# Local attention on one NeuronCore: the product with swapped halves in one VectorE instruction, and the inverse root written straight into the norms' tile

## The chip, the cores and the metric

The program runs on one NeuronCore of a Trainium2 chip, as one launch. The metric is device time in microseconds (us); lower is better. A NeuronCore has four engines that compute: TensorE (PE in the profile; its weight loads are shown apart as PEld), VectorE (DVE), ScalarE (ACT) and GpSimd (POOL). A fifth, SyncE (SP), issues most of the transfers. Each engine takes its own instructions strictly in order; an instruction that waits holds up everything behind it on that engine.

## The reference, cut to what matters

The program is a stack of eight stages (four attention layers, four feed-forward layers) over an activation of 4 sequences x 512 positions x 128 channels, with a residual sum and a layer norm after each stage. The change lies in the second stage alone, a two-layer local attention with eight heads of 64 channels. The part that matters:

```python
def l2norm(t):
    return t / jnp.clip(jnp.linalg.norm(t, axis=-1, keepdims=True), 1e-12)

def rotate_half(x):
    x1, x2 = jnp.split(x, 2, axis=-1)
    return jnp.concatenate([-x2, x1], axis=-1)

def rotary_xpos(q, k):
    ...
    q = q * cos * scale + rotate_half(q) * sin * scale
    k = k * cos / scale + rotate_half(k) * sin / scale
    return (q, k)

def _layer(x, wqkv, qs, ksc, wo, lg, lb, w1, b1, w2, b2):
    ...
    qkv = h @ wqkv
    q, k, v = jnp.split(qkv, 3, axis=-1)
    q, k, v = (to_heads(q), to_heads(k), to_heads(v))
    q = l2norm(q) * qs
    k = l2norm(k) * ksc
    q, k = rotary_xpos(q, k)
    o = local_attention(q, k, v)
    ...
    h = a * jax.nn.gelu(g, approximate=False)
    x = x + h @ w2 + b2
    return x
for l in range(DEPTH):
    x = _layer(x, wqkv[l], q_scale[l], k_scale[l], ...)
```

Queries and keys are divided by their norms, scaled, and rotated: each vector times a cosine table, plus the vector with its two halves of 32 swapped times a sine table.

## The kernel before, in words

The stages run one behind the other on one core, and overlap at their seams: the next stage's loads and first operands are made while the last one ends. Local attention is class `F0`. It works through eight *units* (two layers x four sequences), and in each unit through eight *heads*, so 64 heads in all. Three streams of work are interleaved:

- `qkv(u)` makes the operands of unit u. For each of four chunks of 128 positions it multiplies by the weights of q, k and v (`mm3`, three matmuls each). For q and for k, ScalarE copies the product out of PSUM into a tile (`ta` for q, `kr` for k; line 1616) and squares it into `sq` (line 1619). VectorE then makes the sine product `tb` (line 1623, **two** instructions, one for each half: the output's first half reads the input's second half and the other way round), the cosine product in place (line 1625) and the sum of squares of each head (line 1626). For q the two products are added on TensorE, by two accumulating transposes; for k GpSimd adds them (line 1633), and the sum is transposed later. When all four chunks are through, `rsqrt` turns the 64 sums of squares of each partition into inverse norms, in ten short VectorE steps that each need the one before (lines 342 to 353), and line 1647 copies the result into the tile `rn`. Line 1653 multiplies the keys by it; the queries' norms are applied later, as a scalar of the scores (line 1689).
- `scores` and `score` work off the heads: TensorE makes scores (line 1676), VectorE adds the band mask and takes the minimum (line 1689, four instructions of 128x128 for a head, out to `sm` and `nb`), ScalarE takes the exponential (line 1691, four a head). `turn` transposes and copies (line 1701), `values` multiplies by v (line 1720). `sm` has one buffer (`ns = 1`), so a head's mask has to wait for the exponentials of the head before.
- `post(u)` is what follows the attention of a unit: divide by the sums (line 1753), project (1759), add (1761), shift by transfers (1764 and 281), normalise, and a feed-forward with a Gelu on ScalarE (line 1800, one instruction of 128x1024 and one of 85x512) and a last sum (1817 or 1820).

Exponential and Gelu use different function tables of ScalarE. At each change between them the compiler puts a table load (ACT_TABLE_LOAD in the profile, under the line of the function that needs it).

The order on each engine is not written out by hand. The program yields steps of these streams in turn; each instruction has a priority from its place in the program, and a scheduler that keeps clocks of its own puts the instructions of all streams in one order for each engine when the program is built. A change of an instruction can so move others that it has nothing to do with. `rsqrt` is also called for the layer norms (`norm`, with four columns in place of 64).

Inside the stage, time 243 to 635 us is where the heads are worked off (line 1676 first starts at 243.4 us); before it unit 0's operands are made under the first stage, and behind it the last two `post` run into the third stage, of which some lines appear below (line 276 loads `a1kvs`, line 946 on GpSimd makes `qt`, line 949 on VectorE reduces it).

Of the kernel before, what the change touches and what calls it, by code (L numbers as in the profile page):

```python
# [12 lines left out]
ALU = mybir.AluOpType  # L13
# [3 lines left out]
P = 128  # L17
# [22 lines left out]
class K:  # L40
# [292 lines left out]
        nc.vector.tensor_tensor(l, ps, h.bitcast(F32), ALU.subtract)  # L333
        return h, l, f

    def rsqrt(self, pool, v, n, bufs=2):

        nc = self.nc
        t = pool.tile([P, 3, n], F32, tag=f"rs{n}", name=f"rs{self.uid}", bufs=bufs)
        self.uid += 1  # L340
        y, a, b = t[:, 0, :], t[:, 1, :], t[:, 2, :]
        nc.vector.tensor_scalar(a.bitcast(I32), v.bitcast(I32), 1, None, ALU.logical_shift_right)
        nc.vector.tensor_scalar(y.bitcast(I32), a.bitcast(I32), -1.0, float(0x5F3759DF), ALU.mult, ALU.add)
        nc.vector.tensor_tensor(a, y, y, ALU.mult)
        nc.vector.tensor_tensor(b, a, v, ALU.mult)
        yield
        nc.vector.tensor_scalar(a, b, 0.375, -1.25, ALU.mult, ALU.add)
        nc.vector.tensor_tensor(a, a, b, ALU.mult)
        nc.vector.scalar_tensor_tensor(y, a, 1.875, y, ALU.add, ALU.mult)
        yield  # L350
        nc.vector.scalar_tensor_tensor(a, y, -0.5, y, ALU.mult, ALU.mult)
        nc.vector.tensor_tensor(b, a, v, ALU.mult)
        nc.vector.scalar_tensor_tensor(y, b, 1.5, y, ALU.add, ALU.mult)
        return y

    def norm(self, r, X):
# [456 lines left out]
class Rel(Attn):  # L813
# [28 lines left out]
    def weights(self):  # L842
        k, d, pool = self.k, self.k.d, self.early
        h, l, fill = k.split_w(pool, d["a1_w3"], 384, "a1w", raw=("t1", 2))
        qkv = k.load(pool, d["a1_qkv"], [P, 384], "a1qkv")
        wo = k.load(pool, d["a1_wo"], [P, P], "a1wo")
        bo = k.bcast(pool, d["a1_bo"], P, "a1bo")
        ub = k.bcast(pool, d["a1_uv"][0], P, "a1ub")
        uv = k.load(pool, d["a1_uv"].rearrange("a p -> p a"), [P, 3], "a1uv")
        self.last = k.load(pool, d["c_last"], [P, 1], "a1last")  # L850
        self.w = dict(h=h, l=l, qkv=qkv, o=wo, bo=bo, ub=ub, uv=uv)
        yield from fill
# [640 lines left out]
class F0:  # L1493
# [83 lines left out]
    def qkv(self, u, X, tag="t"):  # L1577

        k, nc, pool = self.k, self.nc, self.more
        own = self.pool if u % 2 else pool  # L1580
        wait = k.turn if u == 0 else lambda: ()
        l, b = divmod(u, NB)
        w = self.w
        xh, xl = self.xs
        if l == 0:
            nc.sync.dma_start(self.x0[b], X)
        yield from k.turn()
        ps = k.bank("b")
        for c in range(4):
            k.tr(ps[:, c * P:(c + 1) * P], X[:, c, :])  # L1590
        yield

        for r, o in ((slice(0, 64), 0), (slice(64, P), 1)):
            nc.scalar.copy(xh[r, o:T + o], ps[r])
            nc.vector.tensor_tensor(xl[r, o:T + o], ps[r], xh[r, o:T + o].bitcast(F32), ALU.subtract)
        qT = own.tile([P, 4, T], F32, tag="qT", name=f"qT{u}")
        kT = own.tile([P, 4, 64 + T], F32, tag="kT", name=f"kT{u}")
        nc.gpsimd.memset(kT[:, :, 0:64], 0.0)
        v = own.tile([P, 4, 512], F32, tag="v", name=f"v{u}")
        kr = pool.tile([P, 4, 512], F32, tag="kr", name=f"kr{u}", bufs=1)  # L1600
        ss = pool.tile([P, 2, 4, 8], F32, tag="ss", name=f"ss{u}", bufs=2)
        for _ in range(2):
            yield
        for c in range(4):
            cs = slice(c * P, (c + 1) * P)
            for s in range(3):
                yield from wait()
                ps = k.bank("b")
                ws = slice(512 * s, 512 * s + 512)
                k.mm3(ps, xh[:, cs], xl[:, cs], w["qkvh"][:, ws], w["qkvl"][:, ws])  # L1610
                if s == 2:
                    nc.scalar.copy(v[:, c, :], ps)
                    yield
                    continue
                x = kr[:, c, :] if s else pool.tile([P, 512], F32, tag="ta", name=f"ta{u}{c}", bufs=self.nta)
                nc.scalar.copy(x, ps)
                yield
                sq = pool.tile([P, 512], F32, tag="sq", name=f"sq{u}{c}{s}", bufs=1)
                nc.scalar.activation(sq, x, AF.Square)
                tb = pool.tile([P, 8, 64], F32, tag="tb", name=f"tb{u}{c}{s}", bufs=2)  # L1620
                x3 = x.rearrange("p (h d) -> p h d", d=64)
                for a, b2 in ((0, 32), (32, 0)):
                    nc.vector.tensor_tensor(tb[:, :, a:a + 32], x3[:, :, b2:b2 + 32],
                                            w["tab"][:, 2 * s + 1, c, None, a:a + 32].to_broadcast([P, 8, 32]), ALU.mult)
                nc.vector.tensor_tensor(x3, x3, w["tab"][:, 2 * s, c, None, :].to_broadcast([P, 8, 64]), ALU.mult)
                nc.vector.tensor_reduce(ss[:, s, c, :], sq.rearrange("p (h d) -> p h d", d=64), AX.X, ALU.add)
                yield
                for _ in range(self.wait_ta if u == 0 else 0):
                    yield
                if s == 0:  # L1630
                    q = x3, tb
                else:
                    nc.gpsimd.tensor_tensor(x3, x3, tb, ALU.add)

            yield from wait()
            t = k.bank(tag)
            for pr in range(4):
                for j, y in enumerate(q):
                    k.tr(t[:, pr * P:(pr + 1) * P], y[:, 2 * pr:2 * pr + 2, :].rearrange("p h d -> p (h d)"), start=(j == 0), stop=(j == 1))
            nc.scalar.copy(qT[:, :, cs], t.rearrange("p (a n) -> p a n", n=P))  # L1640
            yield

        sf = ss.rearrange("p s c h -> p (s c h)")
        nc.vector.tensor_scalar(sf, sf, 1e-24, None, ALU.max)
        rn = pool.tile([P, 2, 4, 8], F32, tag="rn", name=f"rn{u}", bufs=2)
        y = yield from k.rsqrt(pool, sf, 64, 1)
        nc.vector.tensor_copy(rn.rearrange("p s c h -> p (s c h)"), y)
        for _ in range(self.wait_rn - 2):
            yield
        for c in range(5):  # L1650
            if c < 4:
                kc = kr[:, c, :].rearrange("p (h d) -> p h d", d=64)
                (nc.gpsimd if self.pk else nc.vector).tensor_tensor(kc, kc, rn[:, 1, c, :, None].to_broadcast([P, 8, 64]), ALU.mult)
                yield
            if c:
                yield from wait()
                t = k.bank(tag)
                for pr in range(4):
                    k.tr(t[:, pr * P:(pr + 1) * P], kr[:, c - 1, pr * P:(pr + 1) * P])
                nc.scalar.copy(kT[:, :, 64 + (c - 1) * P:64 + c * P], t.rearrange("p (a n) -> p a n", n=P))  # L1660
        self.S[u] = (qT, kT, v, rn)
# [729 lines left out]
```

## Time and profile before

| | |
|---|---|
| median of 3 runs | 2247.07 us (2244.59, 2247.07, 2247.89) |
| the profiled execution's own time | 2249.67 us |
| its span, first to last instruction | 2247.6 us |
| mean granted clock of TensorE | 0.965 |
| VectorE busy in the span | 1669.2 us in 5592 instructions |
| line 1623: count, median duration | 128 (half products of 128x256), 418 ns for q and 416 ns for k |
| line 1625: count, median duration | 64 (128x512), 683 ns for q and 682 ns for k |
| line 1647: count, median duration | 8 (128x64), 193 ns |
| table loads of ScalarE in local attention's heads (243 to 635 us) | 12 (6 for Gelu, 6 for the exponential), 1283 ns each |

All durations are of one profiled execution. A duration runs from an instruction's start to its end; neighbours on VectorE overlap a little, so what an instruction takes of the engine is the distance to the next one's start.

### The profile page before, as it was taken

To read this page: it belongs to the slowest core of one execution; us is meant where nothing else is said; L and a number is where in the kernel's file an instruction comes from. 1 tells how busy PE (TensorE), PEld (TensorE's weight loads), DVE (VectorE), ACT (ScalarE), POOL (GpSimd) and SP (SyncE) were. 2 spreads that over 40 slices of the span, in tenths; PEclk is the share of its full clock that TensorE was granted. 3 is DMA by queue.
4 is the path that set the end of the run, shared out by engine and by line. 5 is a ranking of instruction groups with operands and counts; after the bars stand their busy time and mean duration, and the time that the engine had idled before them with its cause. 6 is when DMAs were issued, how large, how long until landed. Compare 5 with 4: busy or idle time off the path is not lost.

```text
span 2247.6 us, 43130 instructions
## 1 busy us (share of the span) xinstructions
PE 2025.6 (90%) x14400; PEld 1472.7 (66%) x14400; DVE 1669.2 (74%) x5592; ACT 1331.7 (59%) x2982; POOL 504.3 (22%) x707
## 2 busy tenths in 40 slices
PE   7999888888878999999999999998999899999897
PEld 4566566676656667676887665776666566666676
DVE  5778688888878676873777775553877877778787
ACT  3566787777734666665333666332877777777632
POOL 3222212111211532433000322531111111111220
PEclk9999999999988999999999999998999999999999
DMA  5321312021433454321021420603889888888400
GB/s 170 106 77 35 102 49 62 8 48 27 116 113 94 143 157 140 113 79 56 16 66 40 117 78 21 218 17 90 209 213 210 203 196 190 195 206 204 104 5 15
DMA packets 264919, 242.10 MB, mean 108 GB/s; under 512 B 106353, under 2 KB 190619, under 8 KB 263867
## 3 DMA queue, kind: packets, MB, share of 16 engines
q1 hardware_dynamic: 259466, 221.86, 37.0%
q0 software_dynamic: 5232, 17.50, 3.3%
q8 instruction: 115, 1.88, 0.4%
q14 instruction: 106, 0.86, 0.1%
HBM read 103.82 MB, written 74.32 MB: 79 GB/s over the span
## 4 chain that ended last, share of the span: by engine, by line
PE 59%; DVE 17%; ACT 9%; DMA 7%; issue 4%; POOL 2%; SPq 1%; ACTq 0%; POOLq 0%; DVEq 0%
PE t L219 5%; PE s L2113 4%; PE o L737 3%; PE s L688 3%; PE t L721 3%; PE o L1377 3%; PE o L1016 3%; PE b L219 3%; PE b L311 3%; PE o L2009 2%; PE s L311 2%; PE b L313 2%; PE b L312 2%; PE s L313 2%; PE s L312 2%
## 5 line engine op out<-in xcount | busy, mean ns | idle before, releaser
L969 DVE CUSTOM_DVE_ANT_0 junk<-w,a1mask 128x640 bf16<-128x640 f32 x256 | 202.9, 817 | 66.3 <-PE w L967 64.4
L219 PE MATMUL t<-ident,p 128*128 128x128 f32 x1280 | 200.6, 278 | 26.4 <-ACT p L1334 17.3
L765 ACT ACTIVATE Pt<-t 128x384 f32<-128x384 f32 (+1 forms) x384 | 179.6, 528 | 67.4 <-PE t L721 55.7
L219 PEld LDWEIGHTS t<-ident,p 128*128 128x128 f32 x1280 | 151.2, 141 | 83.5 <-ACT p L1334 38.3
L1347 ACT COPY PT<-t 128x512 f32<-128x512 f32 x256 | 149.9, 595 | 76.2 <-PE t L219 75.3
L1043 ACT ACTIVATE Pt<-t 128x512 f32<-128x512 f32 x256 | 149.1, 597 | 73.4 <-PE t L1042 44.4
L1334 ACT ACTIVATE p<-s,nb 128x512 f32<-128x512 f32 x256 | 178.2, 700 | 12.4 <-DVE nb L1333 6.7
L1333 DVE TENSOR_REDUCE nb<-s 128x1 f32<-128x512 f32 x256 | 174.4, 685 | 2.5
L690 DVE CUSTOM_DVE_ANT_0 junk<-s,a0mask 128x128 bf16<-128x128 f32 (+3 forms) x256 | 114.1, 484 | 45.9 <-PE s L688 45.0
L1352 DVE CUSTOM_DVE_ANT_0 jk<-p,a3right 128x496 bf16<-128x496 f32 (+3 forms) x256 | 124.6, 487 | 26.9 <-ACT p L1334 14.8
L690 DVE CUSTOM_DVE_ANT_0 junk<-s,a2mask 128x128 bf16<-128x128 f32 (+3 forms) x256 | 114.8, 483 | 30.5 <-PE s L688 30.4
L774 POOL TENSOR_SCALAR_AFFINE_SELECT Pt<-Pt 128x512 f32<-128x512 f32 x112 | 70.0, 637 | 256.4 <-ACT Pt L765 256.3
L1331 DVE TENSOR_TENSOR s<-s,W 128x160 f32<-128x160 f32 (+1 forms) x256 | 80.9, 317 | 62.5 <-PE s L1329 61.2
L1328 PE MATMUL s<-a3KT,a3QT 128*128 128x512 f32 x256 | 118.7, 466 | 5.6 <-DVE nb L1333 2.5
L1377 PE MATMUL o<-PT,V 128*64 128x512 f32 x512 | 116.9, 598 | 0.5 <-ACT PT L1347 0.5
L1691 ACT ACTIVATE p<-sm,nb 128x128 f32<-128x128 f32 x256 | 100.7, 397 | 24.8 <-DVE nb L1689 24.4
L1329 PE MATMUL s<-a3K,a3Q 128*128 128x512 f32 x256 | 102.1, 400 | 0.0
L1040 PE MATMUL t<-a1Q,a1K 128*128 128x512 f32 (+3 forms) x256 | 92.4, 366 | 6.3 <-ACT Pt L1043 3.9
L1689 DVE CUSTOM_DVE_ANT_0 sm<-s,band,rn 128x128 f32<-128x128 f32 x256 | 78.2, 343 | 26.4 <-PE s L1676 19.3
L688 PE MATMUL s<-a0K,a0Q 128*128 128x256 f32 (+2 forms) x256 | 83.8, 387 | 14.4 <-DVE mx L690 7.3
L966 PE MATMUL w<-a1K,a1Q 128*128 128x256 f32 (+2 forms) x192 | 83.1, 433 | 10.6 <-DVE mx L969 9.7
L1996 ACT ACTIVATE sl<-s 128x512 f32<-128x512 f32 x64 | 37.9, 598 | 91.0 <-PE s L313 85.6
(493 smaller groups left out, 5803.3 us busy)
## 6 DMA issues: line engine op xcount, KB each, us to landing
W<-a3dsk SPq DMA_DIRECT2D x32, 640.0 KB
a1Q<-a1iq SPq DMA_DIRECT2D x32, 512.0 KB
a3dpw<-p SPq DMA_DIRECT2D x64, 160.0 KB
a3dpw<-p SPq DMA_DIRECT2D x64, 144.0 KB
a1K<-a1ik SPq DMA_DIRECT2D x64, 128.0 KB
a3Q<-a3dim SPq DMA_DIRECT2D x32, 256.0 KB
a3QT<-H SPq DMA_DIRECT2D x64, 128.0 KB
a3QT<-L SPq DMA_DIRECT2D x64, 128.0 KB
```

The costliest lines, as they stand in the source:

```text
L219: return self.nc.tensor.matmul(out.bitcast(x.dtype), x, i[:n, :n], is_transpose=True, start=start, stop=stop)
L688: self.scored = nc.tensor.matmul(s[:, :nm], self.qof(0, t, i)[:, qc * P:(qc + 1) * P], Ks[:, i, :nm], start=True, stop=True).ins
L690: nc.vector.tensor_tensor_reduce(junk[:, :n], s[:, :n], k.mask[:, 512 - n:512], 1.0, NEG, ALU.add, ALU.max, mx[:, qc, i:i + 1])
L765: ready = nc.scalar.activation(Pt[:, i, z:], s[:, z:], AF.Exp, scale=sc).ins
L969: nc.vector.tensor_tensor_reduce(junk, s.rearrange("p a n -> p (a n)")[:, T - n:T + m], k.mask[:, T - n:T + m], 1.0, NEG, ALU.add, ALU.max ...
L1043: nc.scalar.activation(Pt[:, i, :T], s, AF.Exp, scale=sc)
L1328: nc.tensor.matmul(s, QT[:, e, qs], KT[:, e, :], start=True, stop=False)
L1333: nc.vector.tensor_reduce(nb, s, AX.X, ALU.min)
L1334: nc.scalar.activation(p[:, e, :], s, AF.Exp, bias=nb, scale=-1.0, accum_out=den[:, qc, 2 * un + e:2 * un + e + 1])
L1347: self.copied[t] = nc.scalar.copy(PT[e][:, :, qc * P:qc * P + P], tb.rearrange("p (c n) -> p c n", n=P)).ins
L1352: nc.vector.tensor_tensor_reduce(jk[:, :nn], p[:, e, x0:], w["right"][:, :nn], 1.0, 0.0, ALU.mult, ALU.add, at[:, e, qc, 31:32])
L1377: m = nc.tensor.matmul(o[64 * e:64 * e + 64, :], V[:, kc, h * 64:h * 64 + 64], PT[e][:, kc, :], start=(kc == 0), stop=False)
```

## The change

The two half products become one VectorE instruction. Output and table are seen as (head, half, 32), and the input as the same with the half axis read backwards. `rsqrt` gets an argument `out`, into which its last step writes; local attention passes the tile `rn`, and the copy goes. The layer norms call `rsqrt` without it, as before.

```diff
-    def rsqrt(self, pool, v, n, bufs=2):
+    def rsqrt(self, pool, v, n, bufs=2, out=None):
...
-        nc.vector.scalar_tensor_tensor(y, b, 1.5, y, ALU.add, ALU.mult)
+        nc.vector.scalar_tensor_tensor(y if out is None else out, b, 1.5, y, ALU.add, ALU.mult)
         return y
...
                 x3 = x.rearrange("p (h d) -> p h d", d=64)
-                for a, b2 in ((0, 32), (32, 0)):
-                    nc.vector.tensor_tensor(tb[:, :, a:a + 32], x3[:, :, b2:b2 + 32],
-                                            w["tab"][:, 2 * s + 1, c, None, a:a + 32].to_broadcast([P, 8, 32]), ALU.mult)
+                nc.vector.tensor_tensor(tb.rearrange("p h (a d) -> p h a d", a=2), x.rearrange("p (h a d) -> p h a d", a=2, d=32)[:, :, ::-1],
+                                        w["tab"][:, 2 * s + 1, c].rearrange("p (a d) -> p a d", a=2)[:, None].to_broadcast([P, 8, 2, 32]), ALU.mult)
                 nc.vector.tensor_tensor(x3, x3, w["tab"][:, 2 * s, c, None, :].to_broadcast([P, 8, 64]), ALU.mult)
...
-        y = yield from k.rsqrt(pool, sf, 64, 1)
-        nc.vector.tensor_copy(rn.rearrange("p s c h -> p (s c h)"), y)
+        yield from k.rsqrt(pool, sf, 64, 1, rn.rearrange("p s c h -> p (s c h)"))
         for _ in range(self.wait_rn - 2):
```

## The prediction

> **What bounds the kernel now.** I read the page's busy shares first, then the same shares by stage, then the groups of instructions of that stage, and last the timelines of VectorE and ScalarE.
>
> ```profile
> PE 2025.6 (90%) x14400; PEld 1472.7 (66%) x14400; DVE 1669.2 (74%) x5592; ACT 1331.7 (59%) x2982; POOL 504.3 (22%) x707
> ```
>
> Over the span TensorE looks like the bound. The table by stage (columns: window, its length, then busy time and count of PE, PEld, DVE, ACT, POOL, then clock, DMA share, GB/s) says something else for the heads of local attention, the second row:
>
> ```profile
> 0.00:243.00 243.00, 209.07 (x1331) 136.15 (x1331) 167.69 (x690) 131.56 (x272) 64.42 (x96) 0.96 0.31 91
> 243.00:635.00 392.00, 327.53 (x3483) 255.96 (x3483) 336.77 (x1205) 300.16 (x867) 76.11 (x85) 0.94 0.23 60
> ```
>
> There VectorE is the busiest (336.8 of 392, 86%), TensorE and ScalarE follow at 84% and 77%. All three hand work to each other in fixed orders, so VectorE sets the pace without being saturated. Unit 0's operands, 8 of the 64 products, are made in the first row, where TensorE leads and VectorE has 69%; I count their saving as nothing, since TensorE covers it (0.6 us if it did not).
>
> **The product.** The two groups of the stage, mean durations behind the bar:
>
> ```profile
> L1623 DVE TENSOR_TENSOR tb<-ta,tab 128x256 f32<-128x256 f32 x56 | 25.2, 486 | 3.8 <-ACT ta L1616 3.5 <-issue 0.3
> L1623 DVE TENSOR_TENSOR tb<-kr,tab 128x256 f32<-128x256 f32 x56 | 21.7, 420 | 1.6 <-ACT kr L1616 1.4
> ```
>
> Durations overlap, so the price is read from start to start:
>
> ```profile
> 262.95 0.68 DVE L1625 TENSOR_TENSOR ta<-ta,tab 128x512 f32<-128x512 f32 x1
> 263.55 0.75 DVE L1623 TENSOR_TENSOR tb<-kr,tab 128x256 f32<-128x256 f32 x2
> 264.22 0.68 DVE L1626 TENSOR_REDUCE ss<-sq 128x8 f32<-128x512 f32 x1
> 264.82 0.68 DVE L1625 TENSOR_TENSOR kr<-kr,tab 128x512 f32<-128x512 f32 x1
> ```
>
> The pair holds VectorE from 263.55 to 264.22, 0.67 us (median over undisturbed pairs: 0.672). The nearest row to the new instruction is line 1625: same 512 elements, same types, the same table broadcast over the heads; it holds VectorE 0.60 us (262.95 to 263.55). So one product saves 0.072 us, and the 56 of the stage save 56 x 0.072 = 4.0 us. No row reads backwards. That the read has gaps costs nothing visible: line 1623 itself reads eight runs of 32, and its 0.336 us a half is just under 0.60 x 1/2 plus one start of about 0.07. I take 0.60; the bound above, if backward reading went at half rate, is 0.60 + 0.53 (the 512 columns once more at the slope (0.60 - 0.336)/256 us, 0.53), which would add 56 x 0.46 = 26 us. The bound below is 0.55, one start less.
>
> The Trainium skill, VectorE: DVE Perf Modes, section The DRAIN you can't avoid, says that the next VectorE instruction does not start until the pipe of the one before is empty. By that the pair would hold 2 x 0.417 and the single 0.683 us, and the estimate of the saving would be 56 x 0.151 = 8.5 us; the rows above, where each next one starts 0.07 to 0.08 us before the end of the one in front, speak for 4.0.
>
> Line 1623's q group has a longer mean (486 ns) than its k group (420). The cause is GpSimd:
>
> ```profile
> 347.87 1.29 POOL L1633 TENSOR_TENSOR kr<-kr,tb 128x512 f32<-128x512 f32 x1 [10.13 <-DVE kr L1625]
> 348.29 1.49 DVE L1623 TENSOR_TENSOR tb<-ta,tab 128x256 f32<-128x256 f32 x2
> ```
>
> The pair takes 1.49 instead of 0.75 us when it starts under a GpSimd addition. Ten of the 128 halves are stretched so, by 4.2 us in all. One long instruction in their place waits as well; I take no change, with 0 to -4.2 us as bounds.
>
> **The root.** The last three steps of a unit, where nothing else lay between:
>
> ```profile
> 594.12 0.22 DVE L353 SCALAR_TENSOR_TENSOR rs<-rs 128x64 f32<-128x64 f32 x1
> 594.37 0.20 DVE L1647 COPY rn<-rs 128x64 f32<-128x64 f32 x1
> 594.60 1.29 DVE L1653 TENSOR_TENSOR kr<-kr,rn 128x512 f32<-128x512 f32 x2
> ```
>
> The copy costs 0.105 us of VectorE where another instruction fills the wait behind it, 0.23 where line 1653 stands right behind. Seven copies in the stage: 0.7 to 1.6 us; I take 0.7. The last step itself only changes its target, at the same size: nothing.
>
> **What moves.** Put side by side, the built orders of the two kernels hold the same instructions but for the above and four table loads on ScalarE, 40 before and 44 after. No transfer is added. Three of SyncE's move; the one that matters is the second layer's table, now behind the four transfers of unit 1's `post`, whose sum stands 1.75 heads later. The table was ready (GpSimd's last work on it) at 373 us and is first needed at 402.7, in unit 4; 10.5 us for the heads and 4 for the transfers fit in these 30, so I count nothing. GpSimd's additions move with the products. From within the third stage on all orders agree again. Inside local attention they differ in 92 stretches on VectorE, 70 on ScalarE and 127 on TensorE, mostly by a place or two.
>
> The loads: in the `post` of units 0 and 3 the two Gelus, back to back before, are now parted by three and two exponentials, so each needs two more loads. A row of the kind:
>
> ```profile
> 387.25 1.28 ACT L1800 ACT_TABLE_LOAD   x1
> 388.54 1.78 ACT L1800 ACTIVATE g<-g 128x1024 f32<-128x1024 f32 x2
> 390.34 1.28 ACT L1691 ACT_TABLE_LOAD   x1
> 391.64 0.40 ACT L1691 ACTIVATE p<-sm,nb 128x128 f32<-128x128 f32 x1
> ```
>
> 4 x 1.283 = 5.1 us on ScalarE. Behind each stand the exponentials, and for them waits VectorE's mask of the next head (`sm` has one buffer). Before, the chain that ended last holds 4 of the stage's 12 loads whole, so a third: 4 x 1.283 x 1/3 = +1.7 us. Bounds 0 (other VectorE work covers it) and 5.1. The Gelu's own delay is covered: after unit 0 its result is needed by unit 4, three units on.
>
> The Trainium skill, ScalarE: Activation LUTs, section What ACT_TABLE_LOAD costs, adds a drain of about 1.38 us to the 1.283, 2.66 us a switch. Here the Gelu starts 1.29 us after its load does, so no such drain shows; by the rule the loads would be 10.6 us on ScalarE and a third of them 3.5, and the estimate of the whole would be 1.8 us slower than mine.
>
> One move I price by itself. Near the last heads, before:
>
> ```profile
> 629.83 0.08 DVE L1689 DVE_READ_ACCUMULATOR2_ANT nb<- 128x1 f32 x1
> 631.53 0.69 DVE L949 TENSOR_REDUCE a1sd<-qt 128x64 f32<-128x512 f32 x1 [1.61 <-POOL qt L946]
> 632.13 0.34 DVE L1689 CUSTOM_DVE_ANT_0 sm<-s,band,rn 128x128 f32<-128x128 f32 x1
> ```
>
> A reduction of the next stage waits 1.61 us for GpSimd (and that for the transfer of `a1kvs`), and the last head's masks and unit 6's residual sum (line 1761, whose transfers come next on the chain) queue behind it. After, line 949 stands behind all masks and behind line 1761. What is freed is 632.13 - 629.83 = 2.3 us, on the chain; bounds 0 (if TensorE's scores come late instead) and 2.3. The masks had no wait of their own there, so I take 2.2.
>
> **The sum.** -4.0 (products) - 0.7 (copies) - 2.2 (line 949) + 1.7 (loads) = -5.2 us. On the profiled execution's own 2249.67 (span 2247.6 and 2.1 around it) that is 2244.5; the median of the runs lies 2.6 below that execution, so I predict **2241.9 us** against 2247.07. 0.2%, 4.5 us, is about what a measurement of this kernel can tell from no change.
>
> **Rivals.**
> - *ScalarE takes the gain* (slower). The four loads are paid whole, because the masks behind them have nothing to run meanwhile, and VectorE's saving turns into longer waits for ScalarE. For it: VectorE's waits right after loads (1.13 us at 393.3, 1.03 at 550.2). Against: ScalarE is at 77%, and only those two of six load pairs show such a wait. 2247.07 + 5.1 = 2252.2; it decides once the loads cost more than 6.9 us less what of the three savings is lost, so with half the savings lost from 3.5 us on.
> - *The order is worse* (slower). In the new order unit 3's last product stands at head 23, before at head 21; a head takes (627.5 - 243.4)/64 = 6.0 us, and unit 3's scores are due at head 24. From a unit's last product to its first scores there go 9.4 us (unit 6: 529.0 to 538.4) to 15.2 us (unit 4: 427.2 to 442.4), for squares, root, key products and transposes. One head covers 6.0 of it, so the heads stand still for 3.4 to 9.2 us; three heads covered all. It decides as soon as other work (unit 1's `post`) doesn't fill that hole: +6, the middle, without the gains: 2253. For it: unit 4's boundary, in the same position now, lies 27.7 us from the scores before it, where others have 7 to 14. Against: unit 1's last product comes half a head earlier, all other units stay within a quarter of a head, and work done in a hole is not due later.
> - *The order is better still*: the waits on GpSimd fall away as well (-4.2) and the loads hide: 2247.07 - 4.0 - 0.7 - 2.2 - 4.2 = 2236.
> - *It is hidden*: TensorE's 84% close up and nothing moves, 2247.
> - *Backward reading is slow*: 2247.07 + 26 - 0.7 - 2.2 + 1.7 = 2272.
>
> **How the numbers follow.** Forecast 0.42 (2237 to 2247: 0.29 faster, 0.12 no change, 0.01 slower); ScalarE 0.18 (0.16 slower, 0.02 no change); worse order 0.20 (0.17 slower, 0.03 no change); better order 0.10, faster; hidden 0.05, no change; slow reading 0.05, slower. Together 0.39 faster, 0.22 no change, 0.39 slower. The range reaches down past the better order, to 2233, by one more wait of the size of line 949's, and up to 2260, the hole at its longest and about half of the loads (9.2 + 2.6 = 11.8, and rounded up). Slow reading and larger swings of the order are left out.
>
> **What would show it.** Right: line 1623's successor with 64 instructions of about 683 ns and 0.60 us from start to start, no line 1647, VectorE busy down by some 5 to 9 us between the first and the last head, and line 1676's first-to-last start (243.4 to 627.5) shorter. Each wrong step has its own row: the product over 0.7 us; new VectorE waits of 1 us or more, ended by line 1691, after loads in units 0 and 3; line 1761 of unit 6 not earlier against the last masks; more than 13.5 us from unit 3's last key product's turn to its scores, or a gap in the heads there. What makes the forecast wrong is the 289 moved stretches: VectorE has some forty waits of 0.5 to 2.6 us in this stage now, and the new order can put such waits in other places.

## The result, and the profile after

The changed kernel is slower. Ten runs of it have a median of 2252.4 us (2247.89 to 2256.19), ten of the kernel before beside them 2243.85 us (2239.06 to 2247.89); the medians lie 8.6 us apart. The ratio on record is 1.0033 with a 95% interval of 1.0021 to 1.0046, so 7.4 us more (4.7 to 10.3); such ratios are used below.

The two profiled executions don't show this in their spans: that of the changed kernel is the shortest of its ten runs (span 2246.1 us), that of before (2247.6 us, an execution of 2249.67) was longer than any of its ten. The difference has to be read inside local attention. In the changed kernel's line numbers the product is line 1622, the cosine product 1624, the scores 1674, the masks 1687, the exponentials 1689, the Gelu 1798 and the product with its result 1805; line 1805 was line 1807. First the busy shares of the page, and the window of the heads in the table by stage (columns as before):

```profile
PE 2019.1 (90%) x14400; PEld 1472.4 (66%) x14400; DVE 1658.9 (74%) x5520; ACT 1335.8 (59%) x2986; POOL 505.5 (23%) x707
```

```profile
243.00:635.00 392.00, 323.24 (x3421) 253.93 (x3420) 325.07 (x1116) 299.46 (x851) 73.70 (x82) 0.94 0.23 59
```

VectorE has 72 instructions and 10.3 us less to do in the whole span (64 half products and 8 copies are gone), as the change says. But in the same 392 us of the heads TensorE has got less done too, 323.2 us where it had 327.5: the heads run later, at the same mean granted clock (0.94 in both rows). The product itself is what it was taken for. The group's lines, then two stretches of VectorE's timeline:

```profile
L1622 DVE TENSOR_TENSOR tb<-ta,tab 128x512 f32<-128x512 f32 x32 | 24.4, 763 | 8.1 <-ACT ta L1616 7.8 <-issue 0.3
...
L1622 DVE TENSOR_TENSOR tb<-kr,tab 128x512 f32<-128x512 f32 x32 | 22.4, 701 | 2.7 <-ACT kr L1616 2.6
```

```profile
263.10 0.67 DVE L1622 TENSOR_TENSOR tb<-kr,tab 128x512 f32<-128x512 f32 x1
263.70 0.34 DVE L1687 CUSTOM_DVE_ANT_0 sm<-s,band,rn 128x128 f32<-128x128 f32 x1
...
266.49 0.68 DVE L1622 TENSOR_TENSOR tb<-kr,tab 128x512 f32<-128x512 f32 x1
267.09 0.68 DVE L1624 TENSOR_TENSOR ta<-ta,tab 128x512 f32<-128x512 f32 x1
```

From its start to the next one's start it takes 0.60 us. Eight of the 64 are stretched, by 3.0 us in all, where the prediction found ten of 128 halves stretched by 4.2 under GpSimd's additions. What has grown is the idle time ahead of it: 4.1 us ahead of all 64 half products of q before, now 8.1. Who waited for whom, on VectorE between 243 and 640 us (columns: who, for whom, us in all, times, longest), before and after:

```profile
DVE sm L1689 <- PE s L1676: 19.3, 10, 6.3
...
DVE sm L1689 <- ACT p L1691: 3.9, 5, 1.1
...
DVE tb L1623 <- ACT ta L1616: 3.5, 5, 1.4
...
DVE a1sd L949 <- POOL qt L946: 1.6, 1, 1.6
```

```profile
DVE sm L1687 <- PE s L1674: 23.9, 13, 6.3
DVE tb L1622 <- ACT ta L1616: 7.5, 8, 2.1
DVE g L1805 <- ACT g L1798: 6.0, 7, 1.3
DVE sm L1687 <- ACT p L1689: 4.7, 7, 1.2
```

The wait of line 949 for GpSimd is gone. In its place masks wait 4.6 us longer for scores, products 4.0 us longer for ScalarE's copies, and line 1805 waits 6.0 us for the Gelu, a row that the kernel before doesn't have. The place where the first two of these waits lie is read from the heads. TensorE makes the scores of two heads at a time, 32 *pairs* in all, four to a unit: pair 8 is unit 2's first, pair 12 unit 3's, pair 16 unit 4's. The time between first starts of the scores, from the trace (us):

| from pair to pair | 0-8 | 8-9 | 11-12 | 8-12 | 12-16 | 16-20 | 20-25 | 25-31 | 0-31 |
|---|---|---|---|---|---|---|---|---|---|
| before | 82.6 | 11.9 | 9.5 | 51.6 | 64.8 | 43.8 | 67.3 | 74.1 | 384.0 |
| changed | 80.4 | 16.4 | 16.8 | 61.1 | 60.9 | 45.5 | 74.6 | 69.5 | 392.0 |

(8-9 and 11-12 are parts of 8-12.) The heads take 8.0 us longer. That is near the loss of the runs, but it is one execution of each kernel: two executions of one and the same order (`f_new_u0old` and `g_u0_dveact` below) differ by up to 2.2 us in such a stretch, so differences of that size say nothing. Of the 8.0 us some come back behind the last scores: at 750 us the changed kernel is 4.9 us behind, where its heads began 0.4 us ahead. The heads gain 2.2 at first, lose 9.5 in pairs 8 to 12, get 3.9 back, lose 1.7 and 7.3 up to pair 25, and get 4.6 back. Two gaps stand out: 8-9, where unit 0's `post` runs, and 11-12, unit 3's boundary. The first one on ScalarE, VectorE and TensorE, before and after:

```profile
334.99 1.28 ACT L1800 ACT_TABLE_LOAD   x1
336.28 1.58 ACT L1800 ACTIVATE g<-g 128x1024 f32<-128x1024 f32 x2
...
338.35 1.28 ACT L1691 ACT_TABLE_LOAD   x1
```

```profile
336.24 0.34 DVE L1689 CUSTOM_DVE_ANT_0 sm<-s,band,rn 128x128 f32<-128x128 f32 x1
...
337.64 0.75 DVE L1807 SCALAR_TENSOR_TENSOR g<-b,b,g 128x512 f32<-128x512 f32 x1 [0.51 <-PE b L313]
```

```profile
337.91 1.10 PE L1676 MATMUL s<-kT,qT 64*64 64x128 f32 x32
```

```profile
333.54 1.28 ACT L1798 ACT_TABLE_LOAD   x1
334.83 1.06 ACT L1798 ACTIVATE g<-g 128x1024 f32<-128x1024 f32 x1
335.91 1.28 ACT L1689 ACT_TABLE_LOAD   x1
337.20 0.40 ACT L1689 ACTIVATE p<-sm,nb 128x128 f32<-128x128 f32 x1
...
338.48 1.28 ACT L1798 ACT_TABLE_LOAD   x1
339.78 0.63 ACT L1798 ACTIVATE g<-g 85x512 f32<-85x512 f32 x1
```

```profile
334.13 0.68 DVE L1595 TENSOR_TENSOR f0xl<-b,f0xh 64x512 fp32r<-64x512 f32 x1
335.92 1.41 DVE L1805 SCALAR_TENSOR_TENSOR g<-b,b,g 128x512 f32<-128x512 f32 x2 [1.12 <-ACT g L1798]
338.50 0.35 DVE L1687 CUSTOM_DVE_ANT_0 sm<-s,band,rn 128x128 f32<-128x128 f32 x1 [1.17 <-ACT p L1689]
...
340.44 0.75 DVE L1805 SCALAR_TENSOR_TENSOR g<-b,b,g 85x512 f32<-85x512 f32 x1 [0.77 <-ACT g L1798]
```

```profile
336.73 0.62 PE L311 MATMUL b<-hfh,w1h 128*85 128x512 f32 x1 [1.94 <-DVE g L1805]
...
339.82 1.99 PE L1674 MATMUL s<-kT,qT 64*64 64x128 f32 x32 [0.76 <-DVE nb L1687]
```

Before, both Gelus run in one piece, masks stand ahead of line 1807, which waits 0.51 us for a product of TensorE and not for the Gelu, and the scores of pair 9 start at 337.91 without a wait. In the changed kernel each engine stands on another one's queue. VectorE stands on the Gelu (1.12), with the next head's masks behind it; these then stand on exponentials (1.17) that ScalarE has put behind the Gelu and a table load; TensorE stands 1.94 us on line 1805, and the scores of pair 9 come behind that and behind the masks (0.76), at 339.82.

The second gap, unit 3's boundary, before and after: the last sine product of its keys on VectorE, and the transposes of the finished keys on TensorE.

```profile
363.62 0.75 DVE L1623 TENSOR_TENSOR tb<-kr,tab 128x256 f32<-128x256 f32 x2
```

```profile
375.27 1.08 PE L219 MATMUL t<-ident,kr 128*128 128x128 f32 x4 [3.30 <-DVE kr L1653]
```

```profile
372.24 0.68 DVE L1622 TENSOR_TENSOR tb<-kr,tab 128x512 f32<-128x512 f32 x1
```

```profile
382.58 1.94 PE L219 MATMUL t<-ident,kr 128*128 128x128 f32 x8 [7.06 <-DVE rs L347]
```

The product stands 8.6 us later, and TensorE waits 7.06 us for what VectorE makes of it, root and keys, where it waited 3.30.

### The profile page after: what moved, and what is told of

It reads as the page before. It is cut to its first block, busy times and chain, and to the rows that moved or that the text cites. A ratio compares the mean times of both kernels' runs of the same rounds, so it can differ in the third digit from the quotient of the medians.

```text
span 2246.1 us, 43050 instructions
## 1 busy us (share of the span) xinstructions
PE 2019.1 (90%) x14400; PEld 1472.4 (66%) x14400; DVE 1658.9 (74%) x5520; ACT 1335.8 (59%) x2986; POOL 505.5 (23%) x707
## 4 chain that ended last, share of the span: by engine, by line
PE 59%; DVE 16%; ACT 11%; DMA 6%; issue 4%; POOL 2%; SPq 1%; ACTq 0%; POOLq 0%; DVEq 0%
PE t L219 5%; PE s L2111 4%; PE o L1377 4%; PE s L688 3%; PE t L721 3%; PE o L737 3%; PE o L1016 3%; PE b L219 3%; PE b L311 3%; PE o L2007 3%; PE b L313 2%; PE b L312 2%; PE s L311 2%; DVE junk L969 2%; PE s L312 2%
## 5 line engine op out<-in xcount | busy, mean ns | idle before, releaser
L219 PE MATMUL t<-ident,p 128*128 128x128 f32 x1280 | 200.2, 278 | 20.2 <-ACT p L1334 13.5
L1347 ACT COPY PT<-t 128x512 f32<-128x512 f32 x256 | 150.2, 595 | 75.2 <-PE t L219 74.1
L690 DVE CUSTOM_DVE_ANT_0 junk<-s,a2mask 128x128 bf16<-128x128 f32 (+3 forms) x256 | 114.9, 484 | 28.6 <-PE s L688 28.4
```

The costliest lines, as they stand in the source:

```text
L219: return self.nc.tensor.matmul(out.bitcast(x.dtype), x, i[:n, :n], is_transpose=True, start=start, stop=stop)
L690: nc.vector.tensor_tensor_reduce(junk[:, :n], s[:, :n], k.mask[:, 512 - n:512], 1.0, NEG, ALU.add, ALU.max, mx[:, qc, i:i + 1])
L1347: self.copied[t] = nc.scalar.copy(PT[e][:, :, qc * P:qc * P + P], tb.rearrange("p (c n) -> p c n", n=P)).ins
```

## The experiments

In most of them the order of instructions is set apart from the instructions. A function at the end of the build ties each instruction of an engine to the one that shall stand ahead of it; the ties add no wait on the chip. With a complete list the build gives exactly the order asked for.

```diff
+def pin(tc, nc):
+    ...
+    for e, code in ORDER.items():
+        ...
+        for a, b in zip(run, run[1:]):
+            tc.add_manual_dep(seen[e][b], seen[e][a].name, mybir.DependencyInfo(mybir.DependencyClass.NoSync, mybir.DependencyReason.DATA), reason="order")
...
         k.run([fs[s] for s in stages], Xs)
+        pin(tc, nc)
```

"Old order" is that of the kernel before, "new order" that of the changed one. Two things in the expectations need a remark: where they say head 7 to head 24 they count pairs, and the unit whose first scores stand at pair 8, which they call unit 1, is unit 2. Ratios are to the kernel before, measured beside each on the same chip, with 95% intervals.

### Instructions and order taken apart

`e_after_oldorder`: the changed instructions, ORDER the old one on all engines.

> The changed instructions (one product with the halves read in reverse, no copy behind the root), on every engine in the order of the kernel before; 40 table loads. Theory 'order' (the moved order costs, the instructions themselves gain): faster than before by the 64 products and 7 copies, 2 to 5 us, so 0.998 to 0.999 of it. Rival 'reading' (the new instruction costs more on the chip than its row says, or holds up a neighbour): as slow as the changed kernel, about 1.003. Rival 'hidden': the saving is covered, 1.000.

`e_before_neworder`: the old instructions, ORDER the new one, the two halves next to each other.

> The instructions of the kernel before (two half products next to each other, and the copy), on every engine in the order of the changed kernel; 44 table loads. Theory 'order': slower than the changed kernel by what products and copies save, so before + 8.5 + 2 to 5 us, 1.004 to 1.006. Rival 'reading': as fast as before, 1.000, or faster by line 949's 2.2 us.

Measured: 0.9988 (0.9980 to 0.9997) and 1.0063 (1.0050 to 1.0076). The changed instructions gain 2.7 us in the old order (0.7 to 4.5), and in the new order 6.7 (1.0063 less 1.0033, about 4 either way). The new order costs 10 us with the changed instructions (6.7 to 13.5) and 14 with the old ones (11 to 17). In the traces TensorE, VectorE, ScalarE and GpSimd follow the order asked for throughout, in both kernels. So theory "order" holds and "reading" falls. The old instructions in the new order also have the gaps of the changed kernel, 16.5 for pairs 8-9 and 17.4 for 11-12.

### The table loads

`e_new_joined` and `f_new_jfront`: the changed kernel, on ScalarE in the `post` of units 0 and 3 (shown for unit 0) the first Gelu behind the exponentials, or the second ahead of them.

```diff
 e_new_joined, ScalarE
-L1798 Gelu, first
 L1689 exponentials x3
+L1798 Gelu, first
 L1798 Gelu, second
 f_new_jfront, ScalarE
 L1798 Gelu, first
+L1798 Gelu, second
 L1689 exponentials x3
-L1798 Gelu, second
```

> The changed kernel in its own order, but in the post of units 0 and 3 the first Gelu stands next to the second again (the exponentials between them go ahead of it); 40 table loads. Theory 'loads' (each parted pair of Gelus holds the heads up by 4 to 5 us): 8 to 10 us faster than the changed kernel, 0.999 to 1.000 of before. Rival 'hole' (unit 3's later last product makes the heads stand still at its boundary): gains at most the four loads' share, 2 us, 1.002 to 1.003 of before.

> The changed kernel in its own order, but in the post of units 0 and 3 the second Gelu goes ahead of the exponentials, right behind the first; 40 table loads. Joining them with the exponentials first gained nothing. Theory 'loads': the parting still costs here, only the late first Gelu hid it; then 5 to 8 us faster than the changed kernel, 1.000 to 1.001 of before (parting them in the old order cost 12 us by the times, 7.8 us by the offset of the instructions behind both posts). Theory 'queues': what costs is that the heads' scores stand behind the Gelu's products on TensorE and the masks behind them on VectorE; then at most 2 us faster, 1.002 to 1.004.

`e_old_split`: `e_after_oldorder` with the second Gelu of unit 0 behind three exponentials and that of unit 3 behind two.

```diff
 e_old_split, ScalarE, unit 0
 L1798 Gelu, first
-L1798 Gelu, second
 L1689 exponentials x3
+L1798 Gelu, second
```

> The changed instructions in the order of the kernel before, but with three exponentials between the two Gelus of unit 0 and two between those of unit 3; 44 table loads. Theory 'loads': 8 to 10 us slower than the same instructions without the parting, 1.002 to 1.003 of before. Rival 'hole': slower than without by 0 to 2 us, 0.998 to 1.000 of before; then the loads are hidden and the rest of the order is what costs.

Measured: joined 1.0029 (1.0017 to 1.0041), second ahead 1.0049 (1.0032 to 1.0066), parted in the old order 1.0043 (1.0030 to 1.0057). The last is 12.4 us slower than the same instructions unparted (0.9988), about 3.6 either way; its pairs 8-12 grow from 50.5 to 55.1 us and 20-25 from 68.2 to 71.3. In the profiled execution, the shortest of its six, all heads take 6.6 us longer (390.6 for 384.0); where the rest of the 12.4 us lies isn't shown. Four loads are 5.1 us. VectorE's waits in that kernel, and its timeline at unit 0's Gelu, show a cost that the loads alone don't have (in `e_after_oldorder` the first of these rows has 0.9 us):

```profile
DVE g L1805 <- ACT g L1798: 7.2, 3, 3.2
```

```profile
335.92 0.75 DVE L1805 SCALAR_TENSOR_TENSOR g<-b,b,g 128x512 f32<-128x512 f32 x1 [0.15 <-PE b L313]
339.79 0.75 DVE L1805 SCALAR_TENSOR_TENSOR g<-b,b,g 85x512 f32<-85x512 f32 x1 [3.12 <-ACT g L1798]
340.57 0.70 DVE L1595 TENSOR_TENSOR f0xl<-b,f0xh 64x512 fp32r<-64x512 f32 x1
341.30 0.35 DVE L1687 CUSTOM_DVE_ANT_0 sm<-s,band,rn 128x128 f32<-128x128 f32 x1
```

VectorE stands 3.12 us on the second Gelu, with a head's masks behind it. So parting costs, and part of it goes through VectorE's queue. But in the new order joining the Gelus brought nothing back; there pairs 8-9 take 17.4 and 19.3 us. In `e_new_joined` the loads are gone and the wait is not: the first Gelu, now behind the exponentials, starts at 336.9 us where it started at 334.8, and VectorE waits 7.0 us for Gelus in all (6.0 in the changed kernel). (In `f_new_jfront` ORDER held only ScalarE, from unit 0's Gelus to unit 3's; the build moved a few places of the other engines there and chose another order from pair 20 on, so its total isn't a clean measure.) So the four loads are not what makes the changed kernel slow, and theory "loads" falls for it; what its waits on the Gelu cost is not settled by these runs.

### Where in the stage

Here ORDER is the new one except in a stretch of pairs.

`f_new_u0old`: the old order in pairs 7 to 10.

> The changed kernel in its own order, but from head 7 to about head 10 (unit 1's first scores, unit 0's post with its Gelus) every engine follows the order of the kernel before. By the offsets the new order loses 5 us there: theory 'local' (each stretch costs by itself what the offsets show) gives 5 us less than the changed kernel, 1.001 of before. Rival 'given back' (the time regained there is lost at the next boundary, since the old order only waits elsewhere): 1.003.

`f_new_postsold`: the old order in pairs 7 to 10 and 13 to 24.

> The changed kernel in its own order, but with the old order in two stretches: from head 7 to head 10 (unit 0's post) and from head 13 to head 24 (units 4 and 5, with unit 3's post). Unit 3's boundary between them and the last heads keep the new order. Theory 'local': 5 + 4.5 + about 1.5 us less than the changed kernel, 0.998 to 0.999 of before, thus all of the loss; unit 3's later last product then costs about 2 us and the last heads give 2 to 3. Rival 'hole' (unit 3's boundary holds the loss): 1.002 to 1.003.

`f_new_b3old`: the old order in pairs 10 to 13.

> The changed kernel in its own order, but from head 10 to head 13 (unit 3's last products, its boundary and its first scores) every engine follows the order of the kernel before. The prediction's rival put 6 us on this place; the offsets show 2.2. Theory 'local': 2 us less than the changed kernel, 1.002 to 1.003. Rival 'hole': 6 us less, 1.000 to 1.001.

`f_old_endnew`: the old order up to about pair 25.

> The changed instructions in the old order, but from about head 25 on (the last heads, with line 949 behind the last masks) in the new order. The offsets show the new order gaining 2.8 us from there to the next stage. Theory 'local': 2 to 3 us faster than the changed instructions in the old order throughout, 0.9970 to 0.9980 of before. Rival 'given back' (the next stage takes the gain): 0.9985 to 0.999.

Ties on a stretch leave the rest to the build, and that moved more than was meant: in `f_new_u0old` pairs 10 to 13 went nearly to the old order as well (in the trace 7 of 468 matmuls and VectorE instructions there stand out of the old sequence, 118 out of the new one); in `f_new_postsold` and `f_old_endnew` the last heads are in a third order, the same in both. `f_new_b3old` differs from the changed kernel only between 359 and 404 us, as was meant.

| kernel | ratio | 8-9 | 11-12 | 8-16 | 16-25 | 25-31 | 0-31 |
|---|---|---|---|---|---|---|---|
| before | 1 | 11.9 | 9.5 | 116.4 | 111.1 | 74.1 | 384.0 |
| changed | 1.0033 (1.0021 to 1.0046) | 16.4 | 16.8 | 122.0 | 120.1 | 69.5 | 392.0 |
| `e_after_oldorder` | 0.9988 (0.9980 to 0.9997) | 11.1 | 9.4 | 115.2 | 112.2 | 74.6 | 384.0 |
| `f_new_u0old` | 0.9994 (0.9980 to 1.0007) | 10.2 | 10.3 | 113.4 | 120.8 | 69.4 | 385.8 |
| `f_new_postsold` | 0.9985 (0.9971 to 1.0000) | 12.4 | 16.9 | 117.7 | 110.0 | 75.3 | 383.0 |
| `f_new_b3old` | 1.0033 (1.0017 to 1.0048) | 16.5 | 9.4 | 122.1 | 120.5 | 69.3 | 392.2 |
| `f_old_endnew` | 1.0018 (1.0004 to 1.0032) | 11.9 | 9.4 | 116.1 | 110.3 | 75.4 | 384.4 |

The largest part sits in pairs 8 to 16: with the old order there 8.6 us of them are back (122.0 to 113.4; 114.8 in a second execution of the same order), and the time is no longer above before (0.9994). Unit 3's boundary alone brings back nothing: the gap of 16.8 us shrinks to 9.4, and 8-16 stays at 122.1, since other pairs in it take as much longer. In pairs 16 to 25 unit 3's `post` loses 9.0 us (120.1 for 111.1), and 25 to 31 give 4.6 of them back; `f_new_u0old` keeps this loss, `f_new_postsold` doesn't (185.3 us for 16 to 31, before 185.2), and the two ratios can't be told apart. By their expectations, `f_new_u0old` regained more than the 1.001 of "local", `f_new_postsold` as much as "local" said, and `f_new_b3old` less than either theory. `f_old_endnew` (1.0018 where 0.997 to 0.999 was expected) is not explained in full: its heads take 384.4 us as they should, but its profiled execution falls behind in the later stages, where its instructions and their order are those of the other kernels (3.2 us ahead of before at 750 us, 1.0 at 760, 6.1 behind at the end). The mean granted clock of its runs is 0.9627, that of `e_after_oldorder` 0.9651; by the estimate in the section on the hardware that is 2.5 of the 6.7 us between them.

### Which engine

`g_u0_pe`, `g_u0_act`, `g_u0_dve`, `g_u0_dveact`: the new order, and in pairs 7 to 10 the old one for the engines named.

> The changed kernel in its own order, but TensorE alone follows the old order from head 7 to head 10: unit 1's last quarter of the first scores ahead of unit 0's feed-forward, its second pair of scores ahead of the third gate product. Theory 'TensorE' (the scores stand too far back in its queue): most of the 8.8 us that the old order of all engines regains, 0.9995 to 1.001. Rival 'VectorE and ScalarE' (the masks and exponentials stand behind Gelu's work, and the scores' banks come free no earlier): 1.002 to 1.004.

> The changed kernel in its own order, but ScalarE alone follows the old order from head 7 to head 10: both Gelus together and behind the exponentials that they stood behind before, two table loads fewer. Theory 'TensorE': 1.002 to 1.004. Rival 'ScalarE': 0.9995 to 1.001.

> The changed kernel in its own order, but VectorE alone follows the old order from head 7 to head 10: the four masks of unit 1's first head ahead of the gate sums. Theory 'TensorE': 1.002 to 1.005, since the masks ahead wait for scores that TensorE still makes late. Rival 'VectorE': 0.9995 to 1.001.

> The changed kernel in its own order, but VectorE and ScalarE both follow the old order from head 7 to head 10, and TensorE keeps the new one. Theory 'TensorE': still slow, 1.002 to 1.005. Rival 'VectorE and ScalarE': 0.9995 to 1.001.

Measured: 0.9986 (0.9975 to 0.9997), 0.9992 (0.9979 to 1.0004), 0.9981 (0.9971 to 0.9991), 0.9987 (0.9974 to 0.9999). All regain everything, and that is no contradiction: with one engine's order tied there the build moved the others back towards the old order too, in this stretch and at unit 3's boundary. `g_u0_dveact` came out as the same order as `f_new_u0old`. `g_u0_pe` and `g_u0_dve` differ in their traces, in 11 short stretches on VectorE and 6 on ScalarE (316 to 322 and 344 to 348 us). In pairs 7 to 10 TensorE follows the old order in all four, but for two matmuls, and ScalarE but for a few places; VectorE in `g_u0_pe` and `g_u0_act` lies between the two orders (11 to 13 of 110 instructions out of the old sequence, 16 to 18 out of the new one). So these runs don't tell TensorE and ScalarE apart, and VectorE's order needn't be wholly the old one. Four orders that nearly agree in pairs 7 to 13, measured five times, lie at 0.9981 to 0.9994, with gaps of 10.2 to 11.1 us for 8-9 and 10.3 to 12.2 for 11-12.

### Which moves

Every engine's order is given in full here: the new one, but for a few moves.

```diff
 h_heads_ahead
   ScalarE:  +L1689 exponentials x3 ahead of both Gelus (were between them)
   VectorE:  +L1687 the second head's 4 masks ahead of L1805 x2 (were behind)
   TensorE:  +L1674 pair 9's scores ahead of the third gate product (were behind it and 2 of L1812)
 h_quarter_ahead
   TensorE:  +L219 the last 4 key transposes and L1674 the last quarter of pair 8 ahead of unit 0's transposes of h
   ScalarE:  +L1658 the copy of these keys ahead of L1783
   VectorE:  +L1687 the first head's 4 masks ahead of L1761 and L1784 (one stood behind them, three behind L1795)
 h_both: all of these
```

> The changed kernel, every engine in its own order but for one group of moves in unit 0's post: three exponentials ahead of the two Gelus, the second head's four masks ahead of the Gelu's products on VectorE, and the second pair's 16 score products ahead of the third gate product on TensorE. Theory 'heads behind Gelu': the second pair's scores start some 3 us earlier (339.8 us in the changed kernel) and most of the 8 us comes back, 0.9995 to 1.001. Rival 'late quarter' (the last quarter of the first scores behind the feed-forward is what counts): 1.0025 to 1.004.

> The changed kernel, every engine in its own order but for one group of moves at unit 1's first head: the last four key transposes, their copy and the last quarter of the scores ahead of unit 0's feed-forward, and the first head's four masks ahead of its split. The Gelus stay parted and where they are. Theory 'heads behind Gelu': three of the first head's exponentials still stand behind the Gelu, so little comes back, 1.002 to 1.0035. Rival 'late quarter': 0.9995 to 1.001.

> The changed kernel, every engine in its own order but for both groups of moves together: unit 1's last key transposes, last quarter of the first scores and first masks ahead of unit 0's feed-forward, and the exponentials, the second head's masks and the second pair's scores ahead of the Gelus and their products. Theory 'the two only work together' (the exponentials can run ahead of the Gelu only once their masks do): from unit 1's first to its second pair of scores some 11 us as in the old order (16.4 in the changed kernel), and 0.9990 to 1.001. Rival 'the rest of the stretch': the first gap shrinks but the next ones grow by as much, 1.002 to 1.004.

Measured: 1.0025 (1.0011 to 1.0039), 1.0043 (1.0028 to 1.0058), 1.0019 (1.0007 to 1.0030). Here the trace holds exactly these moves. The second group alone makes it no better (pairs 8-9 take 18.3 us), so "late quarter" falls; the first group's 1.0025 lies above the 1.001 that "heads behind Gelu" allowed. The first group brings pairs 8-9 from 16.4 to 12.2 us, both together to 12.6; but 9-10 grows from 13.1 to 15.3 in `h_both`, 11-12 stays at 16.7, and 8-16 is 121.1 us against 122.0. The rival "the rest of the stretch" holds for the larger part: the time won at the first place is not kept behind the next one, unit 3's boundary, which these runs left as it was.

### One part of the change at a time

`f_product_only` and `f_root_only`: the kernel before with only the new product, or only the root's new target; the build's own order.

> Only the product is one instruction; the root keeps its copy; the order is what the build makes of it. Its instructions are worth 56 x 0.072 = 4 us by the row. Theory 'order': the built order is a third one, so the time may lie anywhere from 0.998 to 1.005 of before, and it isn't the product's price that tells. Rival 'reading': as slow as the changed kernel or slower, 1.003 or more.

> Only the root's last step writes the norms' tile; the product stays two instructions; the order is what the build makes of it. The copies are worth 0.7 us by the row. Theory 'order': again another order, so anywhere from 0.997 to 1.005, by far more than the copies' price. Rival 'small edit, small effect': 0.999 to 1.000.

Measured: 1.0007 (0.9989 to 1.0026) and 1.0026 (1.0014 to 1.0038). The smaller part alone, a copy of 0.1 us less in each unit, costs 5.8 us (3.1 to 8.5): its build has 14 table loads among the heads where before has 12, gaps of 14.9 us for 8-9 and 17.4 for 11-12, and 121.2 us in 8-16. The product alone has gaps of 11.1 and 11.1 and 114.9 us in 8-16; its time can't be told from before. "Small edit, small effect" falls.

A version that beats both kernels came out of this: the lowest ratio is that of `g_u0_dve`, 0.9981 (0.9971 to 0.9991), about 4 us faster than before and 12 faster than the changed one. It is the lowest of 18 measured, so in part chosen by luck; the changed instructions in the old order, 0.9988, can't be told from it.

## Why the prediction was wrong

*The product.* Right. 0.60 us from start to start was taken and 0.60 is measured; there are 64 instructions, and reading in reverse costs nothing that shows.

The Trainium skill's rule (VectorE: DVE Perf Modes, The DRAIN you can't avoid), as the prediction used it, would have had the next instruction start at the end, 0.67 us after the start; it starts 0.07 us before that, so the row decided rightly. The same section adds that "A next op that is not held starts earlier", which the prediction left out; the trace agrees with that sentence.

*Products and copies, 4.0 + 0.7 us.* Right in sign where the order is held, and near in size: 2.7 us (0.7 to 4.5) in the old order, 6.7 (about 2.7 to 10.7) in the new one. The 4.7 us lie just above the first interval and inside the second.

*Line 949, 2.2 us.* The wait went, as forecast, but less came of it. VectorE's timeline of the changed kernel near the last head:

```profile
638.62 0.35 DVE L1687 CUSTOM_DVE_ANT_0 sm<-s,band,rn 128x128 f32<-128x128 f32 x1 [0.90 <-ACT p L1689]
...
639.44 0.68 DVE L1759 TENSOR_TENSOR X<-X,b 128x512 f32<-128x512 f32 x1
...
640.31 0.68 DVE L949 TENSOR_REDUCE a1sd<-qt 128x64 f32<-128x512 f32 x1
```

Line 949 no longer waits, but a mask ahead of it waits 0.90 us for exponentials. From the last scores' start (635.0) to the residual sum (line 1759) it is 4.4 us, before 5.5: 1.1 us of the 2.2. "The masks had no wait of their own there" was the faulty step: they stood behind one on ScalarE as soon as line 949's was gone.

*The loads, 1.7 us with 5.1 as the upper bound.* Wrong mechanism. "The Gelu's own delay is covered: after unit 0 its result is needed by unit 4" looked at the unit's result and not at the first reader: line 1807 (1805 after) reads the Gelu's output at once, on VectorE, and masks stand behind it in that queue. Where only the parting was added, it cost 12.4 us (8.8 to 16) by the runs, 6.6 of them in the heads of the profiled execution, and not 1.7. In the changed kernel it isn't a separate sum: rejoined, nothing came back.

*Everything else that moved, counted as nothing.* This is the step that failed and turned the sign. In the prediction's sum the whole new order is worth -2.2 + 1.7 = -0.5 us, line 949 and the loads; all other moves stand at nothing, for no better reason than that they are "mostly by a place or two". With the instructions held, the new order costs 10 us with the changed instructions and 14 with the old ones. A place or two is no bound for a queue. Which of the moves does it stays open; most of it lies in pairs 8 to 16. The prediction named the 289 moved stretches as what could make it wrong, but gave a worse order 0.20 and by a single mechanism.

*The rival "the order is worse".* Its time, 2253, lies beside the 2252.4 measured, in part by luck: it is 2247.07 + 6, while the ten runs of before beside the changed kernel have 2243.85. Its hole at unit 3's boundary is there: 16.8 us for 9.5, 7.3 more, within its 3.4 to 9.2 (these rest on 6.0 us a head, which divides by 64 a time that spans 62 heads; it is 6.2). The way from the last product to the scores has not grown, 372.2 to 384.5 us for 363.6 to 377.5; it begins later, as the rival had it. But the hole by itself isn't what costs: taken away alone, the time stayed at 1.0033. The part that it left out is pair 8-9, unit 0's `post`, and that the two places cover for each other: with both gone 8.6 us of 8-16 are back (122.0 to 113.4), with the second alone none, with the first alone 4.3 (117.7 in `f_new_postsold`, where unit 3's boundary is that of the changed kernel, though pairs 13 to 16 have the old order). That one delay hides under the other is read from these sums and not shown by itself; which single move starts it stays open. Exchanging one or two engines' orders in that stretch and holding the rest was not tried.

*The rival "ScalarE takes the gain".* Its 2252.2 (2247.07 + 5.1) is near, too, but the whole price of the loads doesn't explain it, by the rejoined kernels.

## What to carry to other kernels

Where a scheduler orders the instructions, an edit has two prices, its own and that of the order that the build makes of it; measure the edit with the old order held, and the order with the old instructions, before either is believed. A late result is priced from its first reader and from what stands behind that reader, not from when the final result is due. And a hole is worth something only if nothing else holds the same stream: take away all of them, or read the sum over the whole stretch.

## What the runs showed of the hardware

A short wait of TensorE can have an aftermath. Columns as in the table by stage, with the granted clock in the column ahead of the last two; the changed kernel, around the wait of 1.94 us shown above:

```profile
336.00:337.00 1.00, 0.27 (x1) 0.25 (x2) 1.00 (x2) 1.00 (x1) 0.00 (x0) 0.94 0.00 0
337.00:338.00 1.00, 1.00 (x3) 0.59 (x2) 0.33 (x1) 0.99 (x6) 0.00 (x0) 0.50 0.03 8
339.00:340.00 1.00, 0.24 (x5) 0.21 (x8) 0.67 (x6) 0.99 (x2) 0.00 (x0) 0.50 0.00 0
342.00:343.00 1.00, 1.00 (x3) 0.83 (x4) 0.00 (x0) 0.99 (x4) 0.00 (x0) 0.50 0.07 16
```

And in the same execution a longer wait, from 271.0 to 273.5 us:

```profile
271.00:273.00 2.00, 0.01 (x1) 0.00 (x0) 2.00 (x9) 1.83 (x8) 0.62 (x1) 1.00 0.63 185
273.00:274.00 1.00, 0.52 (x17) 0.52 (x19) 1.00 (x4) 1.00 (x4) 0.00 (x0) 1.00 0.57 145
```

TensorE is idle from 334.8 to 336.7, and at 337 the clock is at half, until past 343: line 313 takes 0.63 us there where it took 0.40 at 334. In `f_new_u0old`, without the wait, the clock is 1.00 in all of these windows. So here a wait that TensorE seems to have time for was followed by some 6 us at half clock. The length of the wait doesn't decide it alone: the 2.47 us at 271.0 were not followed by a lower clock, nor was a wait of 1.92 us at 318.4 in `f_new_u0old`. What decides stays open. The Trainium skill (TensorE: Matmul & The Clock Gate, Part 1: The HAM clock gate) has the clock fall after an idle window of about 3.4 us; here it fell with 1.94 us in one piece.

What this costs can be estimated from the record. Between executions of one kernel a mean granted clock lower by 0.001 goes with a span longer by about 1.1 us (an estimate, a line fitted to all executions of the record with one slope). The runs of the changed kernel have a mean of 0.9639, those of `e_after_oldorder` 0.9651, those of `e_before_neworder` 0.9610 and those of before beside these two 0.9651. By the estimate some 1.3 of the 10 us that the new order costs, and 4.4 of the 14, come with the clock; the larger part doesn't. For what the old order brings back in pairs 8 to 16 the share may be larger: the mean clock there is 0.94 in `f_new_u0old`, 0.89 in the changed kernel and 0.90 before.

Also not expected: in three builds the number of moved instructions was no guide to the cost of an order. Counted in the traces, VectorE's order differs from that of before in 89 stretches in `f_root_only`, in 118 in `f_product_only` and in 139 in the changed kernel (products and copies left out); the ratios are 1.0026, 1.0007 and 1.0033.
